# Layer 1 of a four-layer graph network: averages in four 32-column tiles, and both groups of a chunk's feature map together

## The chip, the cores and the metric

The kernel runs on one core of a Trainium2 chip. The metric is the device time of one execution in microseconds (us); the median of several executions is compared. The engines are TensorE (PE, with its weight loads as PEld), VectorE (DVE), ScalarE (ACT), GpSimd (POOL) and SyncE (SP, which issues transfers).

## The reference

A batch of 8 graphs with N = 2048 nodes and 64 features goes through four graph layers, each of the form "normalise, rectify, layer, add to the input". All is float32. The change lies in layer 1 and in the normalisation ahead of layer 2:

```python
h = jnp.maximum(_layernorm(x, axis=-1), 0.0)
x = x + _L1_gnn_ref(h, adj, L1_gnn_W, L1_gnn_a)
...
def _layernorm(x, axis=-1, eps=1e-5):
    m = jnp.mean(x, axis=axis, keepdims=True)
    v = jnp.var(x, axis=axis, keepdims=True)
    return (x - m) / jnp.sqrt(v + eps)
...
def _L1_gnn_ref(input, adj, W, a):
    h = jnp.matmul(input, W)
    s_src = jnp.matmul(h, a_src)
    s_dst = jnp.matmul(h, a_dst)
    e = jax.nn.leaky_relu(s_src[:, :, None] + s_dst[:, None, :], negative_slope=ALPHA)
    mask = adj > THRESHOLD
    attention = jax.nn.softmax(jnp.where(mask[None, :, :], e, NEG_INF), axis=2)
    h_prime = jnp.matmul(attention, h)
    return jax.nn.elu(h_prime)
```

## The kernel before

Two graphs of the batch make a pair, so that their 2 x 64 features fill the 128 partitions; there are NP = 4 pairs. A pair's data lies as 128 partitions by 2048 nodes and is worked on in NCW = 4 chunks of CW = 512 columns, or in NT = 16 tiles of 128 nodes. The adjacency matrix stays in the core's memory for all layers, transposed, as 16 tiles aT (the last four are called aTl).

**Layer 1's attention** (`attend`, L1707) takes one pair, in two halves hf of 1024 receiving nodes. For each of the 16 tiles m of sending nodes, DVE makes two products pt (L1739, one for each graph of the pair): the larger of R and wd, times the adjacency. Then PE uses them twice: `features` (L1718) multiplies them with the features hS into o, in eight matmuls of 32 columns each, four column tiles side by side; `sums` (L1726) does the same with vd for the denominators dn, in four. Even m run features first, odd m sums first, so that two o or two dn groups follow each other. Between the two groups of each m, `between(m)` is called, which is where other work enters PE's order. Six buffers hold pt, three m's worth.

After a half, ACT takes the logarithm and exponential of dn into ds (L1748, L1749), POOL's queue writes ds to d_dram and reads it back, spread over partitions, as den (L1754). At the third `between` of the next half, `end` (L1759) runs: DVE multiplies o by den into res, ACT computes two exponentials e, DVE makes e final, and POOL's queue adds it to the activations in memory. R is loaded from r_dram for each half.

**What enters between.** While pair p is in attention, `neighbour_steps` (L1563) prepares pair p + 1, one chunk after the other, as a generator that is advanced a step at a time. `norm_steps` (L750) gives the first two steps of a chunk. The first: PE multiplies the chunk x by avg (a 128x128 matrix that averages over each graph's 64 features) into mean, DVE subtracts into xc, ACT squares into q. The second: PE multiplies q by avg into var, ACT takes logarithm and exponential, DVE multiplies into xc, which is then the normalised chunk hn. In the third and fourth step PE multiplies two 128-node tiles each by W1x into ph (128 features and four scores per node), and ACT empties ph with six instructions: vd (an exponential), sc (a copy) and four scaled copies into hS. A last step, the tail, makes wd and rs from the scores, turns rs into pr on PE and writes it to r_dram. In accumulator memory (PSUM) this work has two banks: "ln" for mean and var, "h" for ph and pr.

While the last pair is in attention, the first part of layer 2 (`front`, L1861) enters in the same way, at the eight m's of the tuple LATE (4, 7, 9, 12, 14, 17, 19, 22): it calls `norm_steps` for its four chunks, with the mean in "ln" and the variance in "h". The first pair was prepared earlier, by a function of its own that the change leaves as it is.

**Order.** In layer 1 the flag `strict` is set, and PE's instructions then stay in the order in which the program issues them: every matmul goes through the helper at L736 (turns through L743), which is why the profile names these lines. On DVE and ACT a scheduler may place instructions earlier or later, while each engine works through its list in order.

Of the kernel before, what the change touches and what calls it, by code (L numbers as in the profile page):

```python
# [8 lines left out]
FP = mybir.dt.float32  # L9
# [7 lines left out]
P = 128  # L17
# [3 lines left out]
NT = N // P  # L21
CW = 512
# [5 lines left out]
def half(b2):  # L28
    return slice(b2 * 64, (b2 + 1) * 64)


def cols(c, w=CW):
    return slice(c * w, (c + 1) * w)
# [602 lines left out]
class Kit:  # L636
# [97 lines left out]
    def mm(self, *args, **kw):  # L734

        one = self.nc.tensor.matmul(*args, **kw)  # L736
        if self.strict:
            self.tc.keep_in_program_order(one)
# [8 lines left out]
    def use_ln_exp(self):  # L747
        self.tc.keep_in_program_order(self.nc.scalar.preload_act_table_set(LN_EXP))

    def norm_steps(self, dst, src, mean, var, xc, q):  # L750

        nc, mm = self.nc, self.mm
        n = dst.shape[-1] // CW
        for c in range(n):
            mm(mean[:, cols(c)], self.avg, src[:, cols(c)], start=True, stop=True)
        nc.vector.tensor_sub(xc, src, mean)
        nc.scalar.activation(q, xc, AF.Square)
        yield
        for c in range(n):
            if callable(var):  # L760
                var = var()
            mm(var[:, cols(c)], self.avg, q[:, cols(c)], start=True, stop=True)
        nc.scalar.activation(q, var, AF.Ln, bias=self.eps)
        nc.scalar.activation(q, q, AF.Exp, scale=-0.5)
        nc.vector.scalar_tensor_tensor(dst, xc, 0.0, q, op0=OP.max, op1=OP.mult)
        yield
# [775 lines left out]
class Layer1:  # L1542
# [20 lines left out]
    def neighbour_steps(self, p):  # L1563


        kit, sb, ps, Wx = self.kit, self.sb, self.ps, self.kit.W1x
        nc, mm = kit.nc, kit.mm
        x1_dram, r_dram = self.x1_dram, self.r_dram

        keep = self.sb2  # L1570
        sc = sb.tile([P, NT, 4], FP, tag="sc", name="sc", bufs=1)
        vd = keep.tile([P, NT, 2], FP, tag="vd", name="vd")
        wd = keep.tile([P, NT, 2], FP, tag="wd", name="wd")
        hS = None
        for c in range(NCW):
            x = sb.tile([P, CW], FP, tag="x", name="x1", bufs=1)
            nc.sync.dma_start(out=x, in_=x1_dram[p, :, cols(c)])
            mean = ps.tile([P, CW], FP, tag="ln", name="mean")
            var = ps.tile([P, CW], FP, tag="ln", name="var")
            xc = sb.tile([P, CW], FP, tag="xc", name="xc")  # L1580
            q = sb.tile([P, CW], FP, tag="q", name="q", bufs=1)
            hn = xc
            for _ in kit.norm_steps(hn, x, mean, var, xc, q):
                yield
            if hS is None:
                hS = (self.sb2 if p % 2 else sb).tile([P, NT, P], FP, tag="hS", name="hS", bufs=1)
            for g in range(2):
                if g:
                    yield
                ms = slice(4 * c + 2 * g, 4 * c + 2 * g + 2)  # L1590
                ph = ps.tile([P, 2, P + 4], FP, tag="h", name="ph")
                for k in range(2):
                    j = 2 * g + k
                    mm(ph[:, k, :], hn[:, j * P : (j + 1) * P], Wx, start=True, stop=True)
                nc.scalar.activation(vd[:, ms, :], ph[:, :, P : P + 2], AF.Exp, scale=0.2)
                nc.scalar.copy(sc[:, ms, :], ph[:, :, P:])
                for k in range(2):
                    m = ms.start + k
                    for b2 in range(2):
                        nc.scalar.activation(  # L1600
                            hS[:, m, half(b2)], ph[:, k, half(b2)], AF.Copy, scale=vd[:, m, b2 : b2 + 1]
                        )
            yield
        nc.scalar.activation(wd, sc[:, :, 0:2], AF.Exp, scale=0.8)
        rs = sb.tile([P, 2, NT], FP, tag="rs", name="rs", bufs=1)
        nc.scalar.activation(rs, sc[:, :, 2:4].rearrange("p t b -> p b t"), AF.Exp, scale=-0.8)
        pr = ps.tile([2 * NT, P], FP, tag="h", name="pr")
        kit.turn(pr, rs.rearrange("p b t -> p (b t)"))
        rr = sb.tile([2 * NT, P], FP, tag="rr", name="rr", bufs=1)
        nc.vector.tensor_copy(rr, pr)  # L1610
        nc.sync.dma_start(out=r_dram[p].rearrange("b (t n) -> (b t) n", n=P), in_=rr)
        yield hS, vd, wd
# [158 lines left out]
    def run(self, aT, following):  # L1771

        kit, l1 = self.kit, self.l1
        tc, nc = kit.tc, kit.nc
        self.pt = self.lasting.enter_context(tc.tile_pool(name="att_pt", bufs=6, reuse_waits="tile"))
        self.sb2 = sb = l1.enter_context(tc.tile_pool(name="att_sb", bufs=2, reuse_waits="tile"))
        self.ps2 = l1.enter_context(tc.tile_pool(name="att_ps", bufs=2, space=PSUM, reuse_waits="tile"))
        kit.use_ln_exp()  # L1780
        kit.strict = True
        ends, now = [], self.now
        for p in range(NP):
            last = p == NP - 1
            if last:
                self.near.close()
                self.R = l1.enter_context(tc.tile_pool(name="l1_late", bufs=2, reuse_waits="tile"))
            steps = following(self.ps, self.pt, self.lasting) if last else self.neighbour_steps(p + 1)
            after = []

            def between(m):
                if m % NT and ends:
                    ends.pop(0)()

                n = (m in LATE) + 2 * (m == 2 * NT - 1) if last else (2, 0, 1, 0, 1)[m % 5] - (m % 20 == 0)
                for _ in range(n):
                    after.append(next(steps, None))

            for hf in range(2):
                ends = self.attend(aT, p, *now, hf, lambda m: between(hf * NT + m))  # L1800
            if last:
                ends.pop(0)()
            after.extend(steps)
            now = next((r for r in after if r), None)
        ends.pop()()
        kit.strict = False
        l1.close()
# [35 lines left out]
LATE = (4, 7, 9, 12, 14, 17, 19, 22)  # L1843
# [422 lines left out]
```

## Time and profile before

| | us |
|---|---|
| median of three runs | 1931.26 |
| lowest and highest | 1929.91, 1939.18 |
| profiled execution | 1937.11 |
| its span, first to last instruction | 1935.3 |

Busy time over the span, and instructions:

| engine | busy us | instructions |
|---|---|---|
| PE | 1868.5 | 10084 |
| DVE | 1176.9 | 1862 |
| ACT | 460.1 | 1043 |
| POOL | 310.9 | 435 |

The groups that the change concerns (mean and var with the shapes 128x128 by 128x512, two records to a matmul in f32):

```profile
L736 PE MATMUL o<-pt,hS 128*32 128x512 f32 x2048 | 234.7, 593 | 1.7 <-DVE pt L1739 1.6
L736 PE MATMUL dn<-pt,vd 128*32 128x512 f32 x1024 | 122.4, 595 | 0.0
```

In these lines stand the line, engine, operation, output and inputs, shapes and count; then busy time and mean duration in ns; then the engine's idle time before them. A single record of o lasts 593 ns, but 2048 of them are busy for only 234.7 us, as four column tiles run at once. So durations of single matmuls can't be added up; the steps from one group's start to the next one's start can.

### The profile page before, as it was taken

What the parts mean: (1) busy time and instruction counts of PE and PEld (TensorE: products, weight loads), DVE (VectorE), ACT (ScalarE), POOL (GpSimd) and SP (SyncE); (2) the same over time, 40 slices, a digit from 0 to 9 for tenths busy, and PEclk for the clock granted to TensorE, in tenths of its full rate; (3) what the DMA queues carried; (4) which work ended last, traced back from release to release, by engine and by line L of the source; (5) the groups of instructions that cost most, each with busy time, mean ns of one, the idle gap of its engine ahead of it and who ended that gap; (6) DMA issues with size and microseconds to landing.
All of it is one profiled execution on the core that took longest, in us unless ns stands there. A gap on an engine that the chain in (4) does not pass through costs nothing.

```text
span 1935.3 us, 25629 instructions
## 1 busy us (share of the span) xinstructions
PE 1868.5 (97%) x10084; PEld 1142.5 (59%) x10084; DVE 1176.9 (61%) x1862; ACT 460.1 (24%) x1043; POOL 310.9 (16%) x435
## 2 busy tenths in 40 slices
PE   7999999878999999999999999999999999999997
PEld 6877777423323332248775568765577855687653
DVE  8675399767898988973327552446623266523465
ACT  6322355565313131111220101301112201012100
POOL 4111078411000000000002110111200022101122
PEclk9999899989999999999999999999999999999998
DMA  7656376374122212214101112101122011121000
GB/s 215 173 161 190 119 231 170 89 190 108 39 61 50 61 45 56 66 25 115 60 23 25 30 44 71 49 14 26 25 73 60 22 25 30 44 71 50 5 19 12
DMA packets 86371, 142.57 MB, mean 74 GB/s; under 512 B 33800, under 2 KB 34056, under 8 KB 83568
## 3 DMA queue, kind: packets, MB, share of 16 engines
q1 hardware_dynamic: 65200, 83.86, 14.9%
q0 software_dynamic: 21040, 56.98, 12.0%
q8 instruction: 81, 1.33, 0.3%
q14 instruction: 50, 0.41, 0.1%
HBM read 106.85 MB, written 37.09 MB: 74 GB/s over the span
## 4 chain that ended last, share of the span: by engine, by line
PE 73%; issue 15%; DMA 4%; DVE 3%; POOL 2%; ACT 1%; SPq 0%; POOLq 0%; DVEq 0%; ACTq 0%
PE acc L736 33%; PE u L736 15%; PE o L736 5%; PE py L736 3%; PE dn L736 2%; PE pd L736 2%; PE pgs L736 2%; PE acc L1060 2%; DMA iv<-ind_dram 1%; PE mean L736 1%; PE var L736 1%; DMA at<-in_adjT 1%; DVE pt L1739 1%; PE pm L736 1%; DMA den<-d_dram 1%
## 5 line engine op out<-in xcount | busy, mean ns | idle before, releaser
L736 PE MATMUL acc<-aT,parts 128*128 128x512 f32 x1664 | 455.8, 418 | 0.0
L736 PEld LDWEIGHTS acc<-aT,parts 128*128 128x128 f32 x1664 | 306.4, 188 | 107.1 <-issue 51.4
L1739 DVE SCALAR_TENSOR_TENSOR pt<-R,wd,aT 128x1024 f32<-128x1024 f32 x192 | 236.0, 1280 | 14.8 <-DMA R<-r_dram 5.6
L736 PE MATMUL u<-W3f,y 64*128 64x512 f32 x1024 | 241.7, 589 | 0.0
L2141 DVE TENSOR_TENSOR pr<-u,embf 128x512 f32<-128x512 f32 x256 | 170.6, 687 | 109.7 <-PE u L736 102.7
L736 PE MATMUL o<-pt,hS 128*32 128x512 f32 x2048 | 234.7, 593 | 1.7 <-DVE pt L1739 1.6
L736 PEld LDWEIGHTS u<-W3f,y 64*128 64x128 f32 x1024 | 100.8, 187 | 119.1 <-issue 119.1
L736 PEld LDWEIGHTS o<-pt,hS 128*32 128x32 f32 x2048 | 64.7, 110 | 155.6 <-issue 144.7
L736 PE MATMUL u<-W3f,v 64*128 64x512 f32 x512 | 133.5, 596 | 0.0
L2153 POOL TENSOR_TENSOR fold<-fold 128x256 f32<-128x256 f32 x64 | 47.7, 745 | 495.8 <-DVE fold L2152 495.8
L736 PE MATMUL dn<-pt,vd 128*32 128x512 f32 x1024 | 122.4, 595 | 0.0
L1957 DVE TENSOR_TENSOR yb<-py,cb_f 128x512 f32<-128x512 f32 x32 | 22.1, 691 | 159.7 <-PE py L736 159.7
L1060 PE MATMUL acc<-at,Y 128*128 128x512 f32 x384 | 106.3, 419 | 0.0
L736 PE MATMUL acc<-aTl,parts 128*128 128x512 f32 x384 | 98.2, 394 | 0.0
L2145 DVE TENSOR_TENSOR pr<-pr 128x512 f32<-128x512 f32 x128 | 88.1, 688 | 2.2
L2047 POOL TENSOR_TENSOR bq<-bq,xp 128x512 f32<-128x512 f32 x16 | 20.8, 1300 | 425.2 <-ACT xp L2030 425.2
L736 PEld LDWEIGHTS u<-W3f,v 64*128 64x128 f32 x512 | 56.6, 186 | 49.8 <-issue 36.4
L1739 DVE SCALAR_TENSOR_TENSOR pt<-R,wd,aTl 128x1024 f32<-128x1024 f32 x64 | 79.7, 1282 | 10.4 <-PE dn L736 6.2
L736 PEld LDWEIGHTS acc<-aTl,parts 128*128 128x128 f32 x384 | 71.4, 188 | 15.5
L1060 PEld LDWEIGHTS acc<-at,Y 128*128 128x128 f32 x384 | 71.3, 195 | 15.0 <-issue 1.3
L736 PEld LDWEIGHTS dn<-pt,vd 128*32 128x32 f32 x1024 | 30.8, 109 | 73.0 <-issue 69.0
L1971 DVE TENSOR_TENSOR parts<-tp,parts 128x512 fp32r<-128x512 f32 x16 | 11.1, 692 | 84.9 <-ACT parts L1970 84.9
(354 smaller groups left out, 2698.4 us busy)
## 6 DMA issues: line engine op xcount, KB each, us to landing
at<-in_adjT POOLq DMA_DIRECT2D x32, 512.0 KB, 5.3
raw<-in_adjT SPq DMA_DIRECT2D x64, 256.0 KB, 3.4
aT<-in_adjT POOLq DMA_DIRECT2D x12, 1024.0 KB, 5.9
xp<-xd SPq DMA_DIRECT2D x45, 256.0 KB, 3.0
R<-r_dram SPq DMA_DIRECT2D x14, 512.0 KB, 3.8
hlo<-lo_dram POOLq DMA_DIRECT2D x18, 235.1 KB, 3.8
hhi<-hi_dram POOLq DMA_DIRECT2D x18, 235.1 KB, 3.6
hi_dram<-hi SPq DMA_DIRECT2D x16, 264.0 KB, 3.1
```

The costliest lines, as they stand in the source:

```text
L736: one = self.nc.tensor.matmul(*args, **kw)
L1060: mm(acc[p], Y[h][:, m, p, :], at[:, k, :], start=m + h == 0, stop=m == NT - 1 and h == 1)
L1739: nc.vector.scalar_tensor_tensor(pt, R[b2], wd[:, m, b2 : b2 + 1], aT[m][:, s].bitcast(FP), op0=OP.max, op1=OP.mult)
L1957: nc.vector.tensor_tensor(yb, py, bias[:, None, :].to_broadcast([P, 4, P]), op=OP.add)
L1971: nc.vector.tensor_tensor(lo, tp, hi.bitcast(FP), op=OP.subtract)
L2047: nc.gpsimd.tensor_add(bq, bq, xp)
L2141: nc.vector.tensor_tensor(a, u[h], emb[:, i, 8 * w : 8 * w + 8, None].to_broadcast([P, 8, F]), op=OP.mult)
L2145: nc.vector.tensor_add(pr[h], pr[h], a)
L2153: nc.gpsimd.tensor_add(fold[:, :, 0:2, :], fold[:, :, 0:2, :], fold[:, :, 2:4, :])
```

## The change

Three edits. In `norm_steps` each average is four matmuls of 32 output columns, one on each column tile, instead of one of 128. In `neighbour_steps` the four tiles of a chunk's feature map are multiplied in one step, into two banks, the first two in "ln" and the others in "h"; ACT empties them as before. And since a chunk has three steps now and not four, `between` advances the generator at other m's: one step at each m whose remainder by 5 is 0, 2 or 4. On PE's list a chunk's second ph group thus stands one m earlier, beside the first, and the tail's pr two m earlier (m = 20 instead of 22). On DVE, the multiplication into xc at m = 19 stands ahead of res instead of behind it, and the copy of pr four products earlier; the first subtraction of the front stands one product later. On ACT, ds stands behind both groups of hS at m = 15 instead of between them. The lists of SP and POOL are the same.

```diff
+    def averages(self, dst, src):
+
+        for q in range(0, P, 32):
+            self.mm(dst[q : q + 32, :], self.avg[:, q : q + 32], src, start=True, stop=True, tile_position=(0, q))
+
     def norm_steps(self, dst, src, mean, var, xc, q):
 
-        nc, mm = self.nc, self.mm
-        n = dst.shape[-1] // CW
-        for c in range(n):
-            mm(mean[:, cols(c)], self.avg, src[:, cols(c)], start=True, stop=True)
+        nc = self.nc
+        self.averages(mean, src)
         nc.vector.tensor_sub(xc, src, mean)
         nc.scalar.activation(q, xc, AF.Square)
         yield
-        for c in range(n):
-            if callable(var):
-                var = var()
-            mm(var[:, cols(c)], self.avg, q[:, cols(c)], start=True, stop=True)
+        if callable(var):
+            var = var()
+        self.averages(var, q)
         nc.scalar.activation(q, var, AF.Ln, bias=self.eps)
...
-            for g in range(2):
-                if g:
-                    yield
+            phs = [ps.tile([P, 2, P + 4], FP, tag=k, name="ph") for k in ("ln", "h")]
+            for j in range(4):
+                mm(phs[j // 2][:, j % 2, :], hn[:, j * P : (j + 1) * P], Wx, start=True, stop=True)
+            for g, ph in enumerate(phs):
                 ms = slice(4 * c + 2 * g, 4 * c + 2 * g + 2)
-                ph = ps.tile([P, 2, P + 4], FP, tag="h", name="ph")
-                for k in range(2):
-                    j = 2 * g + k
-                    mm(ph[:, k, :], hn[:, j * P : (j + 1) * P], Wx, start=True, stop=True)
                 nc.scalar.activation(vd[:, ms, :], ph[:, :, P : P + 2], AF.Exp, scale=0.2)
...
-                n = (m in LATE) + 2 * (m == 2 * NT - 1) if last else (2, 0, 1, 0, 1)[m % 5] - (m % 20 == 0)
+                n = (m in LATE) + 2 * (m == 2 * NT - 1) if last else m % 5 in (0, 2, 4)
```

## The prediction

> **What bounds the kernel now.** I read the page's busy table and chain first, then the busy time by stretch over layer 1, then TensorE's timeline there, then the list of waits.
>
> ```profile
> PE 1868.5 (97%) x10084; PEld 1142.5 (59%) x10084; DVE 1176.9 (61%) x1862; ACT 460.1 (24%) x1043; POOL 310.9 (16%) x435
> ...
> PE 73%; issue 15%; DMA 4%; DVE 3%; POOL 2%; ACT 1%; SPq 0%; POOLq 0%; DVEq 0%; ACTq 0%
> ```
>
> TensorE (PE) is busy for 97% of the span and carries 73% of the chain of waits. The change touches only layer 1's attention, from 466 us to about 860 us. Its first three pairs, by stretch (columns: stretch, length, busy time and count of PE, weight loads, DVE, ACT, POOL, then PE clock, DMA share, GB/s):
>
> ```profile
> 466.00:565.00 99.00, 98.29 (x814) 30.16 (x818) 88.29 (x78) 22.54 (x70) 2.76 (x4) 1.00 0.21 53
> 565.00:662.00 97.00, 96.31 (x809) 29.57 (x805) 86.33 (x77) 22.53 (x69) 5.52 (x8) 1.00 0.22 53
> 662.00:758.00 96.00, 96.00 (x805) 29.43 (x801) 88.06 (x78) 23.40 (x70) 5.52 (x8) 1.00 0.21 50
> ```
>
> PE leaves under 1 us open in each, at full clock; DVE is second with 8 to 11 us open. TensorE's timeline shows what PE's time goes to (start, length, line, operation, records; an f32 matmul leaves two records, so "x32" of o is 16 matmuls of 32 columns):
>
> ```profile
> 655.30 1.90 PE L736 MATMUL dn<-pt,vd 128*32 128x512 f32 x16
> 657.01 3.62 PE L736 MATMUL o<-pt,hS 128*32 128x512 f32 x32
> 660.45 1.90 PE L736 MATMUL dn<-pt,vd 128*32 128x512 f32 x16
> 662.16 3.62 PE L736 MATMUL o<-pt,hS 128*32 128x512 f32 x32
> 665.71 1.12 PE L736 MATMUL mean<-x,avg_f 128*128 128x512 f32 x2
> 666.76 1.92 PE L736 MATMUL dn<-pt,vd 128*32 128x512 f32 x16
> 668.50 3.62 PE L736 MATMUL o<-pt,hS 128*32 128x512 f32 x32
> ...
> 678.39 0.72 PE L736 MATMUL ph<-W1x,xc 128*128 128x132 f32 x4
> 679.04 1.92 PE L736 MATMUL dn<-pt,vd 128*32 128x512 f32 x16
> 680.90 0.72 PE L736 MATMUL ph<-W1x,xc 128*128 128x132 f32 x4
> 681.45 1.02 PE L736 MATMUL mean<-x,avg_f 128*128 128x512 f32 x2
> 682.40 3.64 PE L736 MATMUL o<-pt,hS 128*32 128x512 f32 x32
> 685.86 1.90 PE L736 MATMUL dn<-pt,vd 128*32 128x512 f32 x16
> ```
>
> Read the steps from start to start. Undisturbed, 16 records of dn take 1.71 (655.30 to 657.01) and 32 of o take 3.44: 0.107 us a record, or **0.858 us for eight records**, four column tiles side by side. A mean between them breaks the pace: the o before it takes 3.55 (+0.11), the mean 1.05, the dn after it 1.74 (+0.03). So a lone full-width mean costs 1.19, a third of a microsecond over its streaming time. The price is per change of width.
>
> ```profile
> DVE pt L1739 <- PE dn L736: 7.4, 11, 1.3
> DVE pt L1739 <- PE o L736: 7.0, 9, 1.1
> PEld o L736 <- DVE pt L1739: 6.8, 11, 1.9
> ...
> 575.36 1.23 DVE L1761 TENSOR_TENSOR res<-o,den 128x1024 f32<-128x1024 f32 x1 [1.97 <-DMA den<-d_dram]
> ...
> 580.83 0.72 PE L736 MATMUL ph<-W1x,xc 128*128 128x132 f32 x4 [0.69 <-DVE xc L765]
> ```
>
> The list of waits over layer 1 (total us, times, longest): DVE waited 14.4 us for PE to free a product tile pt, against 6.8 us the other way, so DVE mostly runs ahead. The last two lines show one place where PE waits: DVE holds at res for den's transfer, is then late with xc, and PE's ph is late.
>
> **What the Trainium skill says.** "TensorEngine Tiling (Array Packing)", Key Properties, states that changing the tiling mode drains TensorE and that different tiles load weights and multiply in parallel. The trace agrees with both: 0.33 us per lone mean over its streaming time, and dn and o at four tiles' pace. "TensorE: Matmul & The Clock Gate", What overlaps and what doesn't, says matmuls are first in, first out, so the last tile's end is the end of all four; no run here shows this apart.
>
> **The change part by part.** Everything is PE time in layer 1.
>
> 1. Means and variances in four tiles: each becomes eight records of the form that dn shows, with 128x512 moving data and 128x32 weights, so 0.858 us and no change of width. The trace has no case of four tiles with the same moving data; in o two tiles share theirs (tiles 0 and 1 read pts[0], 2 and 3 pts[1]) and keep pace. Bounds: 0.858 if they overlap, 3.43 (four times) if they don't. I take 0.858.
> 2. Both ph groups together: the list above prices a lone ph of two matmuls at 0.11 + 0.65 + 0.03 = 0.79, and a ph joined with a mean (680.90 to 682.40, with 0.11 before and 0.02 after) at 1.63. Four records more at 0.11 each (weight loads of a ph row: four in 0.52, the last 0.19 long) make a ph of four matmuls 0.79 + 0.44 = 1.23; with 0.13 a record it would be 1.31.
> 3. Steps: a chunk has three instead of four. By the old schedule steps fall at m = 0, 2, 4, 5 (two), 7, 9, 10 (two) and so on; by the new at m = 0, 2, 4, 5, 7, 9, 10. Means, variances and the first half of ph keep their m; the second half moves one m earlier, and the tail (pr, r_dram) from m = 22 to m = 20. SP's and POOL's orders are unchanged, so no transfer is moved past another; the r_dram write only comes two m (5 us) sooner and is needed at m = 31 or later.
>
> Per pair before: one lone mean 1.19, four variances 4.76, three joined 4.89, five lone ph 3.95: 14.79. After: eight averages 6.86, four ph 4.92: 11.78. Saved 3.0 per pair, **9.0 in three pairs**. The fourth pair's inserts are layer 2's front, which calls norm_steps too: four means and four variances, all lone, 8 x 0.33 = **2.7**. Gross 11.7.
>
> What is taken back. At 580.83 PE already waited for xc, whose start was set by den's landing, which hangs on the end of dn before the mean; the mean and variance between save 0.66, and PE merely waits that much longer: -0.66. In the next pair the same xc is done at 677.4 and PE would come at 678.4 less 0.11 and 0.66, at 677.6: nothing lost. In the fourth pair DVE works without a break from 775.1 to 801.2 after a late den, and PE's dn at 782.18 takes 2.00 instead of 1.72 or so: the 0.33 of the first mean is lost there; afterwards DVE needs 21.3 for eight m (16 products of 1.21, xc and v) against PE's 23.2, so the rest stays. Net 11.7 - 0.7 - 0.3 = **10.7**.
>
> Costed at nothing: the bank "ln" now holds mean, variance and the first ph in turn, and the next mean waits for ACT to empty that ph. ACT starts 0.75 after ph starts and needs 1.15 for a group's six instructions, so the bank is free at 1.9; PE comes to the mean at 1.12 + 1.72 = 2.8. Cover 0.9. On ACT ds now stands behind both groups: it is ready at 2.9 and ACT is free at 3.05, 0.15 later for den. pr at m = 20 needs rs, behind eight hS instructions and, at this half, behind the two e: counted from the last dn of the first half, den lands at 9.2, e ends at 12.6, rs at 15.6, and PE comes at 16.75. Cover 1.1. On DVE, xc now stands ahead of res at m = 19, so a late den no longer holds up xc.
>
> After 865 us PE is busy for 171.0 of the next 171 us and no stretch is set by a fixed transfer, so what layer 1 gives is kept. The profiled execution took 1937.1 us (span 1935.3): it becomes 1926.4. The median of the runs, 1931.26, lies 5.8 below it; the saving is PE's at full clock in both, so 1931.3 - 10.7 = 1920.6.
>
> **The rivals.**
> - *DVE becomes the bound* in the first 20 m of a pair. For: DVE has 54 (four chunks of ten products and two norms), 4.9 (res, e), and 4 to 6 us of waits for R and den, some 64, against PE's new 63. Against: DVE enters with six finished products, 7.7 us of PE work. If the lead goes, half of the pairs' 9.0 is lost: -6, 1925.
> - *den late*: if den lands 3 us later than in the trace, e, hS, rs and then pr hold PE for 2 us a pair, which the old m = 22 covered: -5, 1926. In the trace DVE starts on it 7.5 to 9.9 us after ds ends.
> - *More*: the wait at 580 belongs to one slow transfer (5.7 us for den, where the median of such transfers is 4.1) and is absent elsewhere: -12, 1919.
> - *Slower: four tiles on the same moving data don't overlap.* At averages, each costs up to 3.43 instead of 0.858: 32 x 2.57 = 82, less 10.7: +71, 2002. It decides once an average takes over 0.33 more than dn's pace (32 x 0.33 = 10.7). Against: o's tiles sharing data.
>
> **How the numbers follow.** What a measurement can tell from no change is 0.5%, 9.7 us: 1921.6. My forecast, 10.7 saved, 0.70, of its own range 9 to 12.5 (1918.8 to 1922.3), with 0.54 beyond the bound and 0.16 within. More: 0.05, faster. DVE bound: 0.14, same. den late: 0.06, same. No overlap: 0.05, slower. Together 0.59, 0.36, 0.05. The range leaves out no overlap and, as runs before spread over 9 us, takes a few us of scatter: 1916.5 to 1927.
>
> **What would show it.** Right: mean and var as eight records in about 0.86, o and dn beside them at 3.44 and 1.71; one ph of eight records per chunk at about 1.1; stretches from a pair's first o to the next 3.0 shorter. Wrong: averages of over 1.2 us; "PEld o <- DVE pt" well over 6.8; pr or a mean waiting for ACT.

## The result, and the profile after

The median of six runs is 1924.6 us (1919.0 to 1928.2), beside 1933.4 us of six runs of the kernel before: 8.7 us less by the medians, 9.8 by the means, and a ratio of 0.9949, interval 0.9927 to 0.9972. The profiled execution took 1925.3 us; its span is 1923.5, 11.8 less than before. Not all of that is the change's: the first layer, which it leaves as it is, ended 3.7 us earlier in this execution (layer 1's first o starts at 462.66 instead of 466.34 us). Over the twelve profiles of this study that start lies between 456.8 and 468.6 us, in no order that a change would explain. So parts are compared below from that first o on.

The page's busy table and chain, then the busy time of the first three pairs by stretch (columns as in the prediction):

```profile
PE 1860.3 (97%) x10276; PEld 1167.0 (61%) x10276; DVE 1174.8 (61%) x1862; ACT 459.9 (24%) x1043; POOL 311.2 (16%) x435
...
PE 54%; issue 5%; POOL 1%; DMA 1%; DVE 1%; ACT 0%; POOLq 0%; SPq 0%; DVEq 0%
```

```profile
466.00:565.00 99.00, 99.00 (x909) 32.07 (x905) 90.58 (x81) 22.12 (x69) 4.62 (x7) 1.00 0.21 55
565.00:659.00 94.00, 94.00 (x865) 30.54 (x857) 86.72 (x77) 23.18 (x70) 5.53 (x8) 1.00 0.23 56
659.00:753.00 94.00, 94.00 (x865) 30.38 (x861) 88.57 (x78) 22.67 (x69) 4.31 (x6) 1.00 0.21 50
```

PE has 192 records more and 8 us less busy time. With the same DVE work in it (77 or 78 instructions), a pair's stretch is 94 us long, where it was 96 to 97, and PE is busy through all of it. The chain's shares can't be set against those before: here they add up to 62% of the span, there to 98%, so less of it was followed back. The timeline of TensorE answers to the one of before at the same place, the second pair's end and the third's beginning:

```profile
650.02 1.90 PE L736 MATMUL dn<-pt,vd 128*32 128x512 f32 x16
651.73 3.62 PE L736 MATMUL o<-pt,hS 128*32 128x512 f32 x32
655.17 1.04 PE L736 MATMUL mean<-x,avg_f 128*32 128x512 f32 x8
656.03 1.90 PE L736 MATMUL dn<-pt,vd 128*32 128x512 f32 x16
657.74 3.62 PE L736 MATMUL o<-pt,hS 128*32 128x512 f32 x32
661.18 1.04 PE L736 MATMUL var<-q,avg_f 128*32 128x512 f32 x8
662.03 1.90 PE L736 MATMUL dn<-pt,vd 128*32 128x512 f32 x16
663.75 3.62 PE L736 MATMUL o<-pt,hS 128*32 128x512 f32 x32
667.30 1.17 PE L736 MATMUL ph<-W1x,xc 128*128 128x132 f32 x8
668.39 1.92 PE L736 MATMUL dn<-pt,vd 128*32 128x512 f32 x16
670.13 1.04 PE L736 MATMUL mean<-x,avg_f 128*32 128x512 f32 x8
```

Read from start to start: the mean takes 0.86 (655.17 to 656.03), and the o before it and the dn after it keep 3.44 and 1.71, as if nothing stood between them. Only ph still costs its neighbours something: the o before it takes 3.55, ph 1.09, the dn after it 1.74.

In the table, "layer 1" runs from its first o to the first py, which is layer 2's first product after the front's averages; "rest" runs from there to the end. A pair's column starts at the first mean that enters in it and ends at the first mean of the next; the first starts at the first o, and "front" is the last pair's.

| us | first pair | second | third | front | layer 1 | rest |
|---|---|---|---|---|---|---|
| before | 101.0 | 98.3 | 110.2 | 78.4 | 388.0 | 1081.0 |
| after | 97.9 | 94.6 | 109.9 | 76.2 | 378.6 | 1082.3 |
| less | 3.1 | 3.7 | 0.4 | 2.2 | 9.4 | -1.3 |

The third pair is the odd one: it ought to give 3 like the others. The loss lies at its end, before the front's first mean. PE's, DVE's and POOL's timelines there, before:

```profile
770.03 1.90 PE L736 MATMUL o<-pt,hS 128*32 128x512 f32 x16
772.91 3.11 PE L736 MATMUL o<-pt,hS 128*32 128x512 f32 x16 [0.98 <-DVE pt L1739]
...
770.44 1.23 DVE L1761 TENSOR_TENSOR res<-o,den 128x1024 f32<-128x1024 f32 x1 [3.70 <-DMA den<-d_dram]
...
765.59 1.24 POOL L1754 DMA_DIRECT2D den<-d_dram  x2 [3.35 <-DMA d_dram<-ds]
```

And after:

```profile
756.59 1.90 PE L736 MATMUL o<-pt,hS 128*32 128x512 f32 x16
761.70 3.66 PE L736 MATMUL o<-pt,hS 128*32 128x512 f32 x14 [3.21 <-DVE pt L1738]
```

```profile
759.23 1.23 DVE L1760 TENSOR_TENSOR res<-o,den 128x1024 f32<-128x1024 f32 x1 [5.93 <-DMA den<-d_dram]
```

```profile
748.18 0.61 POOL L1750 DMA_DIRECT2D d_dram<-ds  x1 [31.25 <-ACT ds L1748]
754.18 1.24 POOL L1753 DMA_DIRECT2D den<-d_dram  x2 [5.39 <-DMA d_dram<-ds]
```

DVE stands 5.93 us at res for den, its products come late, and PE waits 3.21 us. Before, the same wait was 3.70 on DVE and 0.98 on PE. The last line of each shows where it starts: the small write to d_dram held POOL for 5.39 us, against 3.35 before. (After such a wait the first mean starts while o still runs, as the last section shows, so up to a microsecond passes between the third column and the front's: in the second profile of the changed kernel, after_again, the two columns are 1.7 and 1.4 less than before instead of 0.4 and 2.2.)

The other loss is in the rest, some 30 us after the first py, in layer 2; the first two lines are of before, the last two of after:

```profile
884.53 1.23 DVE L2071 TENSOR_TENSOR W3f<-W3f 128x1024 f32<-128x1024 f32 x1 [7.11 <-DMA W3f<-in_L_gnn_weight]
...
879.45 1.05 PE L736 MATMUL py<-Wec_f,v 128*128 128x128 f32 x8
...
872.91 1.23 DVE L2070 TENSOR_TENSOR W3f<-W3f 128x1024 f32<-128x1024 f32 x1 [7.06 <-DMA W3f<-in_L_gnn_weight]
...
876.76 1.16 PE L736 MATMUL py<-Wec_f,v 128*128 128x128 f32 x8 [1.17 <-ACT v L2088]
```

DVE stands for layer 3's weights W3f, whose loads took some 16 us from issue to DVE's start on them, against 15 before (869.70 to 884.53); behind it yb, ACT's parts and its v are late, and PE waits. In the profile before, DVE waited 7.1 us too, and PE was not held. Counted from the first py, DVE starts on W3f at 30.1 to 30.5 us in the profiles where it waits for these loads and PE isn't held, and at 31.6 to 32.1 in those where PE is held; PE's wait is what lies beyond 30.5. So before, at 30.2, had 0.3 us to spare.

### The profile page after: what moved, and what is told of

It is laid out like the page before. It is cut to its first block, busy times and chain, and to the rows that moved or that the text cites. A ratio compares the mean times of both kernels' runs of the same rounds, so it can differ in the third digit from the quotient of the medians.

```text
span 1923.5 us, 26014 instructions
## 1 busy us (share of the span) xinstructions
PE 1860.3 (97%) x10276; PEld 1167.0 (61%) x10276; DVE 1174.8 (61%) x1862; ACT 459.9 (24%) x1043; POOL 311.2 (16%) x435
## 4 chain that ended last, share of the span: by engine, by line
PE 54%; issue 5%; POOL 1%; DMA 1%; DVE 1%; ACT 0%; POOLq 0%; SPq 0%; DVEq 0%
PE acc L736 31%; PE u L736 14%; PE o L736 3%; PE py L736 2%; PE dn L736 1%; DMA W3f<-in_L_gnn_weight 1%; PE var L736 1%; PE pv L736 1%; PE mean L736 1%; POOL fold L2152 1%; POOL ot L2153 0%; PE tx L743 0%; PE tp L743 0%; PE tv L743 0%; POOL ot L2154 0%
## 5 line engine op out<-in xcount | busy, mean ns | idle before, releaser
L736 PE MATMUL o<-pt,hS 128*32 128x512 f32 x2048 | 244.5, 595 | 3.8 <-DVE pt L1738 3.8
L736 PEld LDWEIGHTS o<-pt,hS 128*32 128x32 f32 x2048 | 79.1, 110 | 143.2 <-issue 109.8
L736 PE MATMUL dn<-pt,vd 128*32 128x512 f32 x1024 | 131.6, 593 | 0.0
L736 PEld LDWEIGHTS dn<-pt,vd 128*32 128x32 f32 x1024 | 40.1, 110 | 65.4 <-issue 49.4
```

## The experiments

Each kernel starts from the changed one unless said otherwise. Six of the expectations (tiles_only to both) took as their yardstick the time from the first pair's first mean to the first py. A tiled mean starts on its first tile while o still runs on the others, 2.53 us after the first o and not 3.47 as at full width, so that yardstick flatters full-width averages by 0.94. The figures below are from the first o, with the yardstick's own in brackets.

Layer 1 and rest are read from one profile of each kernel; where PE's list is the same they repeat closely (the first pair takes 97.92 us in after, after_again, end_later and w3_kept). The ratios come from the run times. Their intervals are 4 to 9 us wide, so smaller steps from one variant to the next rest on the profiles.

| kernel | layer 1 | (yardstick) | rest | ratio to before, interval |
|---|---|---|---|---|
| before | 388.0 | (384.5) | 1081.0 | |
| after | 378.6 | (376.1) | 1082.3 | 0.9949 (0.9927 to 0.9972) |
| after_again | 378.0 | (375.5) | 1082.3 | 0.9947 (0.9931 to 0.9964) |
| tiles_only | 380.7 | (378.2) | 1082.6 | 0.9980 (0.9970 to 0.9990) |
| ph_only | 386.2 | (382.7) | 1081.1 | 1.0003 (0.9990 to 1.0015) |
| two_tiles | 384.6 | (381.2) | 1081.0 | 0.9993 (0.9982 to 1.0004) |
| end_later | 373.0 | (370.5) | 1082.3 | 0.9943 (0.9924 to 0.9962) |
| ph_tiled | 372.2 | (369.7) | 1080.8 | 0.9932 (0.9912 to 0.9952) |
| both | 371.0 | (368.5) | 1081.1 | 0.9920 (0.9898 to 0.9942) |
| w3_kept | 378.7 | (376.1) | 1080.9 | 0.9964 (0.9952 to 0.9977) |
| best | 371.2 | (368.7) | 1080.7 | 0.9910 (0.9888 to 0.9931) |
| best2 | 369.4 | (366.8) | 1080.9 | 0.9906 (0.9882 to 0.9930) |

**tiles_only: the averages alone.**

```diff
-            phs = [ps.tile([P, 2, P + 4], FP, tag=k, name="ph") for k in ("ln", "h")]
...
+            for g in range(2):
+                if g:
+                    yield
...
-                n = (m in LATE) + 2 * (m == 2 * NT - 1) if last else m % 5 in (0, 2, 4)
+                n = (m in LATE) + 2 * (m == 2 * NT - 1) if last else (2, 0, 1, 0, 1)[m % 5] - (m % 20 == 0)
```

> Averages in four column tiles, ph and the steps as in the kernel before. Yardstick: TensorE's time from the first pair's first mean to the front's first py, 384.5 us before and 376.1 after. Theory (each change of tile width costs 0.33): per pair eight averages at 0.86 and eight lone ph at 0.79 make 13.2 instead of 14.8, so 1.6 less in each of three pairs and 2.7 in the front, 7.5 less: 377 us, if nothing is taken back by waits for den. Rival (the gain came from the two ph groups together and the shorter schedule): no less than 383.

Measured: 7.3 us less in layer 1, for 7.5 expected (378.2 on the yardstick, for 377). In the first pair, where the waits are as before, it is 1.8 for 1.6; after that the wait for xc of the profile before (0.7 us) is gone, and about as much is lost at den. The timeline, where a ph stands between o and dn and another beside a mean:

```profile
663.42 3.62 PE L736 MATMUL o<-pt,hS 128*32 128x512 f32 x32
666.97 0.72 PE L736 MATMUL ph<-W1x,xc 128*128 128x132 f32 x4
667.62 1.92 PE L736 MATMUL dn<-pt,vd 128*32 128x512 f32 x16
669.47 0.72 PE L736 MATMUL ph<-W1x,xc 128*128 128x132 f32 x4
670.12 1.06 PE L736 MATMUL mean<-x,avg_f 128*32 128x512 f32 x8
```

Each of the two ph (0.65 each) now breaks the pace by itself: o before it 3.55, dn between them 1.85. So with tiled averages a split ph changes width twice per chunk. The rival (no gain from the averages) is out. The run times show less: a ratio of 0.998, some 4 us, and 5.8 at the interval's edge. Of the 7.3, 1.6 us are lost in the rest, at W3f.

**ph_only: ph together alone.**

```diff
-        for q in range(0, P, 32):
-            self.mm(dst[q : q + 32, :], self.avg[:, q : q + 32], src, start=True, stop=True, tile_position=(0, q))
+        self.mm(dst, self.avg, src, start=True, stop=True)
```

> ph groups together and three steps per chunk as in the changed kernel, averages full-width as before. Theory: the mean that used to stand beside a ph now stands alone, so per pair eight lone averages 9.5 and four ph 4.9 make 14.4 instead of 14.8: about 1 us less in all, 383.5 on the yardstick. Rival (the two parts add): the 8.5 us of the changed kernel less what tiles_only gives, or, if ph together is the main part, 377 to 380.

Measured: 1.8 us less in layer 1, some 0.7 of it the wait for xc in the second pair, which only the profile before has; the ratio shows no difference. The two parts don't add up: in the first pair, which no wait for den touches, they give 1.8 (tiles_only) and 0.3 (ph_only) alone and 3.1 together. They are not independent: with full-width averages, parting ph from the mean costs a change of width and joining the two ph saves one, so the count hardly moves. With tiled averages, joining the two ph saves a change of width in every chunk.

**two_tiles: averages in two tiles of 64 columns.**

```diff
-        for q in range(0, P, 32):
-            self.mm(dst[q : q + 32, :], self.avg[:, q : q + 32], src, start=True, stop=True, tile_position=(0, q))
+        for q in range(0, P, 64):
+            self.mm(dst[q : q + 64, :], self.avg[:, q : q + 64], src, start=True, stop=True, tile_position=(0, q))
```

> As the changed kernel, but each average in two tiles of 64 columns. Theory A (any change of tile shape has to drain the array): about 1.19 us for each lone average as with full width, 383 to 384 on the yardstick. Theory B (only a full-width instruction waits for all tiles, narrower ones flow in tile by tile): 0.86 to 0.9 each, 376 to 377.

```profile
592.67 3.62 PE L736 MATMUL o<-pt,hS 128*32 128x512 f32 x32
596.22 1.08 PE L736 MATMUL var<-q,avg_f 128*64 128x512 f32 x4
597.23 1.92 PE L736 MATMUL dn<-pt,vd 128*32 128x512 f32 x16
598.97 3.62 PE L736 MATMUL o<-pt,hS 128*32 128x512 f32 x32
```

The o before takes 3.55, the average 1.01, the dn after 1.74: 1.15 in all, against 1.19 at full width and 0.86 in tiles of 32. It is the change of tile shape that costs, not the full width: theory A. (Layer 1 takes 381.2 us on the yardstick, below the 383 to 384 of theory A: each of 32 averages costs 0.04 less than the 1.19 assumed, and the wait for xc is gone here too.) The Trainium skill, "TensorEngine Tiling (Array Packing)", Key Properties, says the same: a change of tiling mode drains the array. The price here is 0.29 us from 64 and 0.33 from 128 columns, there and back.

**end_later: res three m later.**

```diff
-        return [lambda: None, lambda: None, end]
+        return [lambda: None] * 5 + [end]
```

> As the changed kernel, but end (res, e and the add to memory) is called at the sixth instead of the third m of a half. Theory (the changed kernel's missing 3 us are DVE standing at res for den at the last two pair boundaries): TensorE's 3.2 us wait before the last pair's first mean goes and the waits at ph after a boundary with it, 371 to 373 on the yardstick. Rival (DVE's total is now the bound, so a wait moved appears elsewhere): 375 to 376.

Measured: 370.5 on the yardstick, half a microsecond below the range, and 5.6 us less than after; the third pair's column falls from 109.9 to 104.9. The ratio, 0.9943 beside after's 0.9949, doesn't show the 5.6 us. At the same boundary, with d_dram as slow as in after (5.06 us):

```profile
754.50 3.62 PE L736 MATMUL o<-pt,hS 128*32 128x512 f32 x32
757.93 1.04 PE L736 MATMUL mean<-xp,avg_f 128*32 128x512 f32 x8
```

The o is whole and followed at 3.43 by the mean: no wait. So the whole of PE's wait there was DVE standing at res for den, and DVE's total is not the bound.

**ph_tiled: the last change of width out.**

```diff
-                mm(phs[j // 2][:, j % 2, :], hn[:, j * P : (j + 1) * P], Wx, start=True, stop=True)
+                for q in range(0, P, 32):
+                    at = j * P + q
+                    mm(phs[j // 2][q : q + 32, j % 2, :], hn[:, at : at + 32], Wx, start=True, stop=True, tile_position=(0, q))
```

> As the changed kernel, but ph too in four column tiles: sixteen matmuls of 32 output columns in place of four of 128. Theory (only the change of width costs): the 0.34 of each of twelve ph goes, 4 us less than the changed kernel, 372 on the yardstick; ph then takes about 0.9. Rival (with 132 columns to stream a record is too short, and each pays a floor of its own): 32 records at 0.06 or more are 1.9 us a ph, 8 us more than the changed kernel.

```profile
596.99 3.62 PE L736 MATMUL o<-pt,hS 128*32 128x512 f32 x32
600.42 1.08 PE L736 MATMUL ph<-W1x,xc 128*32 128x132 f32 x32
601.32 1.90 PE L736 MATMUL dn<-pt,vd 128*32 128x512 f32 x16
```

ph takes 0.90 and the o before it 3.43; the 0.06 us a record of the rival stands in no trace here. The first two pairs are each 1.3 to 1.4 us shorter than in after (four ph of 0.34). Layer 1 is 6.4 us shorter, where 4 were expected (369.7 on the yardstick, for 372): the other 2.4 are not ph's doing, since here d_dram took 3.23 us and PE waited 0.81 instead of 3.21.

**both** joins the two edits.

> ph in four column tiles and end at the sixth m of a half. If both theories hold, 367 to 369 on the yardstick, 16 us less than before; if DVE's total is the bound, 372 or more, since its products and norms are the same.

Measured: 368.5 on the yardstick, within the range, 16 us less than before and 1.2 less than ph_tiled. The first two pairs are 0.6 longer than in ph_tiled: PE waits 0.57 at pr in each of three pairs. best's timeline below shows why.

**after_again: is the slow transfer scatter?** The file is the changed kernel's.

> The changed kernel once more. Theory A (the two slow transfers in its profile, 5.4 us until d_dram is written at the last pair boundary and 15.7 us for W3f, are scatter from run to run): a second profile shows 3.2 to 3.4 and about 14, TensorE waits 0.8 to 1.0 us instead of 3.2 before the front, and from the first o to the first py it is 376.2 instead of 378.6. Theory B (they come with the changed kernel's timing): the same waits again, 378.6.

```profile
752.44 1.24 POOL L1753 DMA_DIRECT2D den<-d_dram  x2 [5.05 <-DMA d_dram<-ds]
```

5.05 us again, PE's wait 2.96, layer 1 at 378.0 and W3f late again (rest 1082.3): theory B. Over all profiles the wait for d_dram at this boundary is 4.0 to 5.4 us in after, after_again, tiles_only, end_later and w3_kept, the five with averages in tiles of 32 and ph at full width, and 3.2 to 3.4 in the other seven.

The traces show what goes with it. Transfers at this boundary, in after and then in ph_tiled (for the queue q8 its packets, MB and share; for the others count, size of each and median us from issue to landing):

```profile
q8 instruction: 1, 0.02, 0.6%
...
xp<-xd SPq DMA_DIRECT2D x2, 256.0 KB, 4.6
...
d_dram<-ds POOLq DMA_DIRECT2D x1, 8.0 KB, 5.4
```

```profile
xp<-xd SPq DMA_DIRECT2D x2, 256.0 KB, 3.1
...
d_dram<-ds POOLq DMA_DIRECT2D x1, 8.0 KB, 3.3
```

In every profile SP issues the two loads of xp 0.1 and 0.5 us after the write, and the write is reported as landed only when the loads are nearly through. In the five slow profiles a packet of 16 KB on the queue called "instruction" falls among the loads as well. In after it runs from 3.38 to 4.32 us after the write's issue; eight of the loads' 256 packets start only then, one after the other from 4.33 us on, and end at 5.45, while the write lands at 5.42. Of the other seven profiles, five have no such packet there, and in two (before, ph_only) it starts at 3.3 to 3.4 us, when the loads are done at 3.4 to 3.5. The other seven boundaries say the same: of their 84 writes in twelve profiles, 71 land after 1.7 to 1.9 us, and each of the 13 that took 2.0 to 3.5 has such a packet, begun between 0.2 us before and 1.1 us after the write's issue. So a slow write goes with an instruction packet at the wrong moment. No run moves that packet alone, so this is read from the traces and not shown by an experiment, and what sets its moment is open. For W3f it is not enough: the five have such a packet during its loads, but so has two_tiles, where they land in time.

**w3_kept: W3f's two operations in program order.**

```diff
-        nc.vector.tensor_sub(W3[:, 0, :], W3[:, 0, :], W3[:, 2, :])
-        nc.vector.tensor_scalar(W3[:, 2, :], W3[:, 2, :], 2.0, None, op0=OP.mult)
+        tc.keep_in_program_order(nc.vector.tensor_sub(W3[:, 0, :], W3[:, 0, :], W3[:, 2, :]))
+        tc.keep_in_program_order(nc.vector.tensor_scalar(W3[:, 2, :], W3[:, 2, :], 2.0, None, op0=OP.mult))
```

> As the changed kernel, but DVE's two operations on W3f stay in program order, some 50 us later, so that DVE doesn't stand for the W3f transfer. Theory (that wait cost TensorE 1.4 us in the third accumulation of layer 2): the time from the first py to the end is 1080.8 to 1081.0 whatever the transfer takes, against 1082.3 in the changed kernel's profile. Rival (TensorE's loss there has another cause): 1082.3 again where the transfer is slow.

DVE reaches W3f at 915.84 without a wait, and the rest is 1080.9, though the loads land as late as in after: the 1.4 us were DVE standing for W3f. The ratio doesn't show it: 0.9964, with an interval that meets after's.

**best and best2.** best is both with end at the eighth m and w3_kept's edit; best2 is best with end at the sixth m again and the tail at m = 22:

```diff
-                n = (m in LATE) + 2 * (m == 2 * NT - 1) if last else m % 5 in (0, 2, 4)
+                n = (m in LATE) + 2 * (m == 2 * NT - 1) if last else m != 20 and m % 5 in (0, 2, 4)
```

> ph in four column tiles, end at the eighth m of a half so that its two e stand clear of hS and pr on ACT, and W3f in program order. From the first o to the first py: 371.0 of the kernel with ph in tiles and end at the sixth m, less the three waits of 0.57 at pr: 369 to 369.5, 18.5 us less than before; ratio about 0.990. Rival (end at the eighth m runs into other work on DVE): 371 or more.

```profile
527.24 1.06 ACT L1768 ACTIVATE e<-e 128x1024 f32<-128x1024 f32 x1
528.21 0.92 ACT L1604 ACTIVATE hS<-ph,vd 128x64 f32<-128x64 f32 x4
...
530.14 0.27 ACT L1610 ACTIVATE rs<-sc 128x32 f32<-128x32 f32 x1
...
530.47 0.28 PE L743 MATMUL pr<-ident_f,rs 128*32 128x128 f32 x1 [0.57 <-ACT rs L1610]
```

The expectation for best failed, with 371.2 for 369 to 369.5: the waits at pr are still there. The rival's number came true, but not its reason. The scheduler put e on ACT between sc and hS as in both, two m later in the program or not, so rs ends late and pr at m = 20 waits. The place in the program doesn't bind ACT's order; only PE's is bound.

> As best (ph in four column tiles, a later end, W3f in program order), with end at the sixth m again and the tail with pr at m = 22 instead of 20. Theory (pr at m = 20 comes 0.57 us before ACT has rs ready, since ACT does the two e first): the three waits at pr go, 1.7 us less than best's 371.2 from the first o to the first py, 369.5. Rival (r_dram is then written too late for the next pair's R): a new wait of products for R, 371 or more.

Measured: 369.4 for 369.5 expected, no wait at pr, rest 1080.9. best2 is 18.6 us shorter in layer 1 than before, and its median is 1916.4 beside 1934.5, ratio 0.9906 (0.9882 to 0.9930). Its interval overlaps after's by a hair and those of ph_tiled, both and best widely, so its lead over these rests on the profile.

## Why the prediction was right

The forecast was 10.7 us less, a ratio of 0.9945. Measured: 0.9949 and 0.9947 in two measurements, and in the profile 9.4 us in layer 1 and 8.1 to the end. The saving lies at the lower edge of the 9 to 12.5 us that were given to it. The time itself, 1924.6 us, is 4.0 above the forecast of 1920.6; 2.1 of that is the kernel before, whose median is 1933.4 over six runs and was 1931.3 over three.

- **The bound** was read rightly: where PE's waits stayed the same, as in the first pair, its time fell by what its list lost (3.1 for 3.0).
- **Averages in tiles**: 0.858 predicted, 0.86 measured, with four tiles on the same moving data. The slower rival is out. Their worth alone is shown by tiles_only; that the change of shape is what costs, by two_tiles.
- **ph together**: 1.23 predicted, 1.23 measured (0.11 before, 1.09, 0.03 after).
- **3.0 per pair**: the first gave 3.1. The second gave 3.7, for the wait of 0.7 at ph was gone. The prediction had that wait grow by 0.66, having taken den's landing in one execution as fixed; den came earlier here (res started at 567.28 without a wait), as the rival "more" had it.
- **The front**: 2.7 less 0.3 predicted, 2.2 measured, and 1.4 in the second profile; the column's start is blurred by the wait ahead of it.
- **The step that failed** is "what is taken back" at the last pair's boundary. It counted 0.33 for a mean there and took PE's wait of 1 us before it as unchanged. The stretch is 2.5 us longer (the two pieces of that o take 8.4 us instead of 5.9): den comes later, d_dram's write having taken 2.0 us more. end_later shows that res standing for den is the whole of PE's wait. The rival "den late" had such a delay, but expected it to be paid at pr, where nothing waited.
- **"No stretch is set by a fixed transfer" after layer 1** was wrong by 1.4 us: DVE starts on W3f 31.7 us after the first py instead of 30.2, and PE loses nearly all of that, so before had next to no slack there (0.3 us), which a busy PE did not show. w3_kept shows that this wait is the cause.
- **Covers** held: no mean waited for the bank "ln", and pr waited only where e was moved and ph shortened too (both, best); with one of the two alone (end_later, ph_tiled) it did not.

The errors were of both signs and cancelled in part: +1.4 at ph (0.7 gained where 0.66 was to be lost), -2.5 at den, -1.3 at W3f. That the sum came out 2.6 us from the profile's 8.1, and not further, is partly luck; the terms for PE's own time were not.

## What to carry to other kernels

Where matmuls in narrow column tiles run back to back, a matmul of another tile shape among them costs about a third of a microsecond above its streaming time (0.29 to 0.34 us here, in float32), so cast the odd ones in the same tiles; read that price from start to start of the neighbours, not from durations. Price a combination and not its parts: how many changes of shape are left depends on who stands beside whom. And after shortening the busiest engine, go through the transfers that another engine stands for in its queue: those waits of one execution, and their covers, are the least certain terms.

## What was not expected of the hardware

- Tiles drift apart. After a wait, the records of the first mean, of o and of dn no longer start in the order of PE's list, though that order is fixed. The mean's first two records start at 765.02, while the last two of the o ahead of it start at 765.19 (lines below). It looks as if each tile went on with a queue of its own; the records don't name their tile, so that is a reading. For starts, the "first in, first out" that the prediction took up does not hold here. Ends are modelled in a profile and say nothing on it.
- A small write (8 KB) lands after 1.7 to 1.8 us in most cases, after 3.2 to 3.4 with two loads of 256 KB issued behind it, and after 4.0 to 5.4 when a 16 KB packet of the instruction queue falls among these too.
- 32 records of 128x32 by 128x132 took 0.90 us, 0.028 each. That is 0.107 times 132/512, so no floor is to be seen.

```profile
765.02 0.60 PE L736 MATMUL mean<-xp,avg_f 128*32 128x512 f32 x2
765.19 0.60 PE L736 MATMUL o<-pt,hS 128*32 128x512 f32 x2
```
